# Attention on one core: two of ten probability chunks turned in 32x32 squares by VectorE and carried over DRAM, and the last query chunk weighed last

## The chip, the core and the metric

The kernel runs on one core of a Trainium2 chip. TensorE (PE in the profile; PEld is its weight load) multiplies into PSUM, VectorE (DVE) and ScalarE (ACT) read PSUM and SBUF, GpSimd (POOL) works on SBUF, and SyncE (SP) issues most of the transfers; the transfers run on 16 DMA engines. The metric is the device time of one execution in microseconds. The kernel before takes 2644.55 us, the median of three runs from 2643.07 to 2644.7.

## The reference

Everything is float32. A layer norm of x (4 batches of 512 tokens, 1024 wide) feeds an attention and a linear layer with routed low-rank additions; both are added to x. The attention has 32 query heads in 8 groups that share keys and values, head width 128, a causal mask, and a bias of minus slope times the root of the distance:

```python
xn = _layernorm(x)
qkv = xn @ w_qkv                      # q: 32 heads, k and v: 8 heads, 128 wide
scores = einsum('bqhgd,bkhd->bhgqk', q, k) * D ** -0.5
bias = -slopes * sqrt(max(rel, 0)), -inf where rel < 0      # rel = query - key
attn = softmax(scores + bias)
out = einsum('bhgqk,bkhd->bqhgd', attn, v).reshape(B, S, NH * D)
x = x + out @ w_o + (xn @ W.T + b + routed_low_rank(xn))
```

## The kernel before

There are three stages. *Projection* (`project`) makes q, k and v with two nested levels of a seven-product scheme for matrix multiplication and leaves them in DRAM. *Attention* (`attend`) works on them and writes its output, again as sums for such a scheme, to DRAM tensors `s`. *Finish* multiplies these by `w_o` and the linear layer's weights. The change is in attention.

Attention has 32 units (p, h, bi): two pairs of batches p, eight groups h, and within them the two batches bi of the pair. A unit has 4 heads and 512 tokens, cut into 4 chunks of 128. Query chunk i sees key chunks j = 0 to i, so a unit has ten (i, j) chunks. For each query chunk there are these steps:

- `scores(u, i)`: for each of the 4 heads, one product of queries by keys into one of three PSUM banks (L1014 on PE, (i+1)*128 columns); VectorE adds the bias, scales and finds the row's minimum (L1019); ScalarE takes exp and the row sum (L1023); VectorE inverts the sums (`tot`, L1026); GpSimd multiplies the rows `p3` to `p0` by them (L1028).
- `transpose_probs(u, i)`: each chunk (i, j) takes four 128x128 transposes on PE into one PSUM bank (L1039, `ptr`) and an eviction to a tile `pt`, by VectorE for even j (L1042) and by ScalarE for odd j (L1044).
- `weigh(u, i)`: PE multiplies the i+1 chunks by the values, 512 columns each (L1052), and ScalarE copies the result into `o` (L1053).
- `values(u)`: four transposes of the values (L1003).

One loop of the program handles a unit u and interleaves it with the scores of the next unit. Its order on PE is written out by hand: scores of the next unit for i=3, transposes of u for i=3; the same for i=2, then the next unit's values; scores i=1, weigh(u,3), transposes i=1; scores i=0, weigh(u,2), transposes i=0; weigh(u,1), weigh(u,0). The last unit has no next one; there a few products of the finish stage (`begin`) are put between.

When a pair of units (bi=0 and bi=1) is done, its outputs are summed for the finish stage: `outer_sums` makes three tiles `os` and one in place of `o`, four sums of 128x1024 on POOL (L130 and L133), done in the bi=0 loop of the next h. `middle_sums` then makes sums `ot` of them: of the `o` of bi=1 on POOL, in the same bi=0 loop, for the tensors (7, 4); of `os` on VectorE, for (5, 6, 3); of the `o` of bi=0 on VectorE, for (1, 2). Each set goes to DRAM by SP (L1105, L1106, L1116, L1118, L1119). For the last h but one `outer_steps` makes the `os` sums on VectorE.

`load` brings keys, queries and values (k, q, vT; L973 to L975) two units ahead. The orders of SP, VectorE, ScalarE and POOL in this stage are not written by hand: they come from the scheduler that builds the program and are fixed in it, an instruction after another for each engine. The tiles `p3` and so on exist twice, `pt` ten times, `o` four times, `os` once.

`homes[0]` is a pool of tiles of the finish stage, laid out already during attention; its tile `s1` (128 x 5 x 256) is used by operand sums of the finish stage.

Of the kernel before, what the change touches and what calls it, by code (L numbers as in the profile page):

```python
# [12 lines left out]
F32 = mybir.dt.float32  # L13
# [8 lines left out]
P = 128  # L22
NH, NKV, D = 32, 8, 128
G = NH // NKV
# [41 lines left out]
def kernel(  # L66
# [13 lines left out]
    nc = tc.nc  # L80
    B, S, H = x.shape
# [5 lines left out]
    HS = S // 2  # L87
    SCALE = D ** -0.5
    KB = 5
# [12 lines left out]
    dram = ctx.enter_context(tc.tile_pool(name="scratch", bufs=1, space=bass.MemoryType.DRAM))  # L102
# [837 lines left out]
            assert not (soon or later or weights or quiet or any(apart))  # L940


    def attend(front, begin):


        early = pool("bq", side="right")
        with ExitStack() as stack:
            sb, sq = None, early.__enter__()
            units = [(p, h, bi) for p in range(NP) for h in range(NKV) for bi in range(2)]
            sizes = {"dist": (S,), "q": (G, S), "k": (S,), "vT": (S,), "bias": (G, S)}  # L950
            counts = {"q": 2, "k": 2, "vT": 2, "v": 2, "pt": 10, "o": 4, "ot": 2}
            for i in (3, 2, 1, 0):
                sizes[f"p{i}"] = (G, (i + 1) * P)
                counts[f"p{i}"] = 2
            sizes.update(v=(NT, D), pt=(S,), os=(3, 2, S), o=(G, S), ot=(9, HS))
            queries = ("dist", "q", "k", "vT", "bias")

            def buf(tag, name):
                where = sq if tag in queries else sb
                return where.tile([P, *sizes[tag]], F32, tag=tag, name=name, bufs=counts.get(tag, 1))  # L960

            Q, K, VT, V, PR, O, bias = {}, {}, {}, {}, {}, {}, {}

            def label(u):
                return "_".join(str(k) for k in u)

            def load(u, queue=nc.sync):
# [19 lines left out]
                out=dist, in_=dist, compare_op=ALU.is_ge, fill=FAR,  # L987
# [10 lines left out]
            def values(u):  # L998
                n = label(u)
                V[u] = buf("v", f"v_{n}")  # L1000
                tr = bank("tr", f"v_{n}")
                for t in range(NT):
                    nc.tensor.transpose(tr[:, ts(t, P)], VT[u][:, ts(t, P)], ident)  # L1003
                nc.scalar.copy(V[u], tr.rearrange("p (t d) -> p t d", d=D))

            def scores(u, i):
                p, h, bi = u
                n = (i + 1) * P
                m = f"{label(u)}_{i}"
                tot = sb.tile([P, G], F32, tag=f"tot{i}", name=f"tot_{m}", bufs=2)  # L1010
                pr = PR[u, i] = buf(f"p{i}", f"p_{m}")
                for g in range(G):
                    sc = bank("sc", f"{m}_{g}")
                    nc.tensor.matmul(  # L1014
                        sc[:, :n], Q[u][:, g, ts(i, P)], K[u][:, :n], start=True, stop=True
                    )

                    low = sb.tile([P, 1], F32, tag=f"low{g}", name=f"low_{m}_{g}", bufs=2)
                    nc.vector.tensor_tensor_reduce(  # L1019
                        pr[:, g], sc[:, :n], bias[p, h][:, g, S - n :], -SCALE, BIG,  # L1020
                        ALU.add, ALU.min, low,
                    )
                    nc.scalar.activation(  # L1023
                        pr[:, g], pr[:, g], AF.Exp, bias=low, scale=-1.0, accum_out=tot[:, g : g + 1]
                    )
                nc.vector.reciprocal(tot, tot)  # L1026
                for g in range(G):
                    nc.gpsimd.tensor_scalar(  # L1028
                        pr[:, g], pr[:, g], tot[:, g : g + 1], 1.0, ALU.mult, ALU.mult
                    )  # L1030

            PT, OS = {}, {}

            def transpose_probs(u, i):
                for j in range(i + 1):
                    m = f"{label(u)}_{i}_{j}"
                    tr = bank("tr", m)
                    for g in range(G):
                        nc.tensor.transpose(tr[:, ts(g, P)], PR[u, i][:, g, ts(j, P)], ident)  # L1039
                    pt = buf("pt", f"pt_{m}")  # L1040
                    if j % 2 == 0:
                        nc.vector.tensor_copy(pt, tr)  # L1042
                    else:
                        nc.scalar.copy(pt, tr)  # L1044
                    PT[i, j] = pt

            def weigh(u, i):
                if u not in O:
                    O[u] = buf("o", f"o_{label(u)}")
                po = bank("o", f"{label(u)}_{i}")  # L1050
                for j in range(i + 1):
                    nc.tensor.matmul(po, V[u][:, j, :], PT[i, j], start=(j == 0), stop=(j == i))  # L1052
                nc.scalar.copy(O[u][:, :, ts(i, P)], po.rearrange("p (g k) -> p g k", k=P))  # L1053
# [87 lines left out]

            for tag in "ot os o p3 p2 p1 p0 v pt".split():
                buf(tag, f"lay_{tag}")
            for i in (3, 2, 1, 0):
                scores(units[0], i)
                if i == 3:
                    values(units[0])
            for n, u in enumerate(units):
                p, h, bi = u
                nxt = units[n + 1] if n + 1 < len(units) else None  # L1150
                after = units[n + 2] if n + 2 < len(units) else None
                if after:
                    load(after)
                if n == len(units) - 6:
                    front[0]()
                if not nxt:
                    early.__exit__(None, None, None)
                    front[1](O[p, h, 0])
                    fill = begin()
                if bi == 1:  # L1160
                    beside.append(middle_sums(p, h, (1, 2), "o", O[p, h, 0], True))
                for i in (3, 2, 1, 0):
                    if nxt:
                        scores(nxt, i)
                    if i > 1:
                        aside(outer, 1)
                    aside(below, 2)
                    if i < 2 or not nxt and i < 3 or n == close - 2 and i == 2:
                        aside(beside, 2)
                    if i < 2:  # L1170
                        weigh(u, i + 2)
                        if i == 0 and not nxt:
                            outer_sums(p, h, slice(HS, S))
                        next(fill, None)
                    transpose_probs(u, i)
                    next(fill, None)
                    if i == 2 and nxt:
                        values(nxt)
                    if i == 3:
                        aside(outer, 1)  # L1180
                    if not nxt:
                        if i == 3:
                            aside(beside, 2)
                        if i == 2:
                            while beside:
                                aside(beside, 1)
                        if i < 2:
                            front[3 - i]()
                if after and after[2] == 0:
                    distances(after)  # L1190
                aside(beside, 2)
                weigh(u, 1)
                next(fill, None)
                weigh(u, 0)
                if n == close:

                    while beside:
                        aside(beside, 1)
                for _ in fill:
                    pass  # L1200
                if bi == 1:
                    if n + 1 == close:
                        o = O[p, h, 1]
                        outer.append(outer_steps(p, h))
                        aside(outer, 1)
                        t = OS[p, h]
                    else:
                        o, t = outer_sums(p, h, slice(0, HS if (p, h) == last else S))
                        beside.append(pause(3))
                        for k in range(2):  # L1210
                            O.pop((p, h, k))
                        OS.pop((p, h))
                    below.append(middle_sums(p, h, (7, 4), "o", o, False))
                    beside.append(middle_sums(p, h, (5, 6, 3), "os", t, False))
# [427 lines left out]
    homes, begun = [], {}  # L1642
# [36 lines left out]
    with tc.manual_schedule(engines={PE, SP}):  # L1679
        attention = attend(  # L1680
            (
                lambda: bring(0, "w", *QUARTERS[:3]), second_home,
                lambda: (ops[1].weights(1), ops[1].weights(2)), lambda: ops[1].tokens(1),
            ),
            begin,
        )
        project(lambda: next(attention))
    with tc.manual_schedule(engines={PE}):
# [42 lines left out]
```

## Time and profile before

| | us |
|---|---|
| median of three runs | 2644.55 |
| the profiled execution | 2642.97 |
| its span, first to last instruction | 2641.2 |
| granted TensorE clock | 0.999 |

| stretch (us) | length | PE busy | DVE busy | ACT busy | POOL busy | DMA share | GB/s |
|---|---|---|---|---|---|---|---|
| 200 to 600 (projection) | 400 | 391.4 | 294.5 | 52.4 | 328.1 | 0.83 | 279 |
| 600 to 1080 (projection) | 480 | 475.7 | 334.5 | 34.1 | 411.5 | 0.72 | 246 |
| 1200 to 1400 (attention) | 200 | 198.6 | 136.0 | 135.7 | 149.8 | 0.67 | 218 |
| 1800 to 2641 (end of attention, finish) | 841 | 827.9 | 534.7 | 46.1 | 533.1 | 0.80 | 290 |

An engine's busy time is the time in which it had an instruction under way. The DMA share is the mean busy share of the 16 DMA engines. In timelines and groups, `po<-pt,v` reads "tile po written from tiles pt and v", x8 is eight instructions, and SPq stands for SP's queue, which issues transfers. A transfer's landing is the time from its issue until its data are there.

### The profile page before, as it was taken

How to read it: one execution, taken by the hardware profiler on the slowest of the kernel's cores; microseconds unless marked ns; L12 is line 12 of the kernel's file. 1: busy time of each engine (PE TensorE's matmuls, PEld its weight loads, DVE VectorE, ACT ScalarE, POOL GpSimd, SP SyncE). 2: the span in 40 equal slices, each digit the busy share in tenths (PEclk: the TensorE clock that was granted, in tenths of full speed). 3: DMA queues.
4: the chain of work that ended last, by engine and by line, in shares of the span. 5: the costliest groups of instructions: out<-in, count | busy, mean ns of one | idle time of the engine just before them, and what ended most of it. 6: DMA issues, size and time to landing. Idle time of an engine off the chain costs nothing.

```text
span 2641.2 us, 35979 instructions
## 1 busy us (share of the span) xinstructions
PE 2592.3 (98%) x11872; PEld 2069.8 (78%) x11872; DVE 1799.8 (68%) x3654; ACT 651.7 (25%) x1730; POOL 1924.0 (73%) x1976
## 2 busy tenths in 40 slices
PE   7999999999999999999999999999999999999999
PEld 6888888888888888856666665656788888888887
DVE  7776867867676677656666666676766666656574
ACT  3111111100000000366766766665000000000000
POOL 3687888877898988666877777684765566755593
PEclk9999999999999999999999999999999999999999
DMA  4479897869876776436566666757987878878884
GB/s 148 135 268 309 305 316 258 275 200 330 275 261 216 240 255 207 144 105 223 189 222 215 209 223 195 233 208 240 369 276 285 310 294 318 296 275 310 308 329 164
DMA packets 386570, 656.19 MB, mean 248 GB/s; under 512 B 22441, under 2 KB 291113, under 8 KB 376274
## 3 DMA queue, kind: packets, MB, share of 16 engines
q1 hardware_dynamic: 314322, 566.47, 61.8%
q10 hardware_dynamic: 70752, 82.85, 9.7%
q0 software_dynamic: 1312, 4.59, 0.5%
q8 instruction: 95, 1.56, 0.2%
q14 instruction: 89, 0.73, 0.1%
HBM read 392.72 MB, written 261.10 MB: 248 GB/s over the span
## 4 chain that ended last, share of the span: by engine, by line
PE 67%; POOL 3%; DVE 3%; DMA 2%; issue 1%; SPq 0%; ACT 0%; POOLq 0%; DVEq 0%; ACTq 0%
PE pc L1310 16%; PE psc L1014 9%; PE po L1052 9%; PE pd L1310 8%; PE pc_q L553 6%; PE pa L1310 4%; PE pc_kv L553 3%; PE ptr L1039 3%; PE pd_q L553 3%; PE pd_kv L553 2%; PE pa_q L553 1%; DVE p L1019 1%; DVE pt L1042 1%; PE pa_kv L553 1%; DMA s<-os 1%
## 5 line engine op out<-in xcount | busy, mean ns | idle before, releaser
L1028 POOL TENSOR_SCALAR p<-p,tot 128x256 f32<-128x256 f32 (+3 forms) x512 | 320.5, 648 | 136.8 <-DVE tot L1026 87.3
L1014 PE MATMUL psc<-k,q 128*128 128x512 f32 (+3 forms) x1024 | 306.2, 437 | 3.4 <-DVE low L1019 2.1
L1019 DVE CUSTOM_DVE_ANT_0 p<-psc,bias 128x256 f32<-128x256 f32 (+3 forms) x512 | 244.6, 490 | 93.6 <-PE psc L1014 71.2
L1023 ACT ACTIVATE p<-p,low 128x256 f32<-128x256 f32 (+3 forms) x512 | 283.8, 555 | 74.6 <-DVE low L1019 61.3
L1052 PE MATMUL po<-pt,v 128*128 128x512 f32 x640 | 290.9, 593 | 0.5 <-DVE pt L1042 0.5
L133 POOL TENSOR_TENSOR t<-w 128x640 f32<-128x640 f32 x95 | 186.3, 1961 | 135.6 <-DMA w<-m 58.9
L1014 PEld LDWEIGHTS psc<-k,q 128*128 128x128 f32 x1024 | 172.6, 190 | 102.7 <-issue 54.3
L133 POOL TENSOR_TENSOR t<-w,t 128x640 f32<-128x640 f32 x95 | 197.3, 2077 | 34.2 <-PE pc L1310 30.5
L1039 PEld LDWEIGHTS ptr<-ident,p 128*128 128x128 f32 x1280 | 147.3, 141 | 71.4 <-issue 40.1
L1052 PEld LDWEIGHTS po<-pt,v 128*128 128x128 f32 x640 | 116.6, 190 | 109.6 <-issue 99.6
L133 POOL TENSOR_TENSOR wr<-wr 128x256 f32<-128x256 f32 x220 | 173.1, 789 | 33.2 <-DMA wr<-in_w_o_dram 10.3
L1042 DVE COPY pt<-ptr 128x512 f32<-128x512 f32 x192 | 130.0, 683 | 75.8 <-PE ptr L1039 73.8
L1039 PE MATMUL ptr<-ident,p 128*128 128x128 f32 x1280 | 167.6, 274 | 4.3 <-DVE pt L1042 2.9
L553 PE MATMUL pc_q<-xi,ti_q 128*128 128x256 f32 x640 | 165.7, 381 | 2.9 <-DVE q L130 1.8
L168 ACT COPY m<-pc 128x256 f32<-128x256 f32 x30 | 11.2, 373 | 562.7 <-PE pc L1310 488.7
L133 DVE TENSOR_TENSOR wr<-wr 128x256 f32<-128x256 f32 x220 | 141.8, 645 | 7.6 <-DMA wr<-in_w_o_dram 4.0
L133 POOL TENSOR_TENSOR ti_q<-w_q 128x256 f32<-128x256 f32 x128 | 106.1, 829 | 56.0 <-PE pc_kv L553 32.9
L553 PEld LDWEIGHTS pc_q<-xi,ti_q 128*128 128x128 f32 x640 | 119.6, 190 | 24.5 <-issue 7.8
L553 PE MATMUL pd_q<-xi,ti_q 128*128 128x256 f32 x448 | 116.0, 381 | 5.6 <-POOL ti_q L133 5.6
L1310 PE MATMUL pc<-sa,w 128*128 128x256 f32 x480 | 113.8, 385 | 4.5 <-DMA sa<-s 4.5
L168 ACT COPY q<-pc_q 128x256 f32<-128x256 f32 x64 | 23.8, 372 | 357.1 <-PE pc_q L553 309.1
L1310 PE MATMUL pd<-s,w 128*128 128x256 f32 x480 | 111.5, 379 | 0.4 <-DVE s L133 0.4
(343 smaller groups left out, 6003.5 us busy)
## 6 DMA issues: line engine op xcount, KB each, us to landing
sa<-s SPq DMA_DIRECT2D x98, 640.0 KB, 8.1
s<-ot SPq DMA_DIRECT2D x107, 384.0 KB, 4.8
m<-wr SPq DMA_DIRECT2D x70, 512.0 KB, 4.7
w<-m SPq DMA_DIRECT2D x28, 1280.0 KB, 7.2
w_q<-in_w_qkv_dram SPq DMA_DIRECT2D x16, 2048.0 KB, 12.2
q<-q SPq DMA_DIRECT2D x32, 1024.0 KB, 7.2
s<-os SPq DMA_DIRECT2D x45, 512.0 KB, 4.8
t<-wr SPq DMA_DIRECT2D x40, 512.0 KB, 4.2
```

The source lines that it names most:

```text
L133: return eng.tensor_tensor(dst, u, v, ALU.subtract)
L168: nc.scalar.copy(dst, src)
L553: nc.tensor.matmul(dst, ops_w[m][:, c, :], XI[i][m][:, c, :], start=start and c == 0, stop=c == 1, skip_group_check=True,)
L1014: nc.tensor.matmul(sc[:, :n], Q[u][:, g, ts(i, P)], K[u][:, :n], start=True, stop=True)
L1019: nc.vector.tensor_tensor_reduce(pr[:, g], sc[:, :n], bias[p, h][:, g, S - n :], -SCALE, BIG, ALU.add, ALU.min, low,)
L1023: nc.scalar.activation(pr[:, g], pr[:, g], AF.Exp, bias=low, scale=-1.0, accum_out=tot[:, g : g + 1])
L1028: nc.gpsimd.tensor_scalar(pr[:, g], pr[:, g], tot[:, g : g + 1], 1.0, ALU.mult, ALU.mult)
L1039: nc.tensor.transpose(tr[:, ts(g, P)], PR[u, i][:, g, ts(j, P)], ident)
L1042: nc.vector.tensor_copy(pt, tr)
L1052: nc.tensor.matmul(po, V[u][:, j, :], PT[i, j], start=(j == 0), stop=(j == i))
L1310: nc.tensor.matmul(bk, w[:, k], x[:, k], start=start and k == 0, stop=stop and k == KB - 1, skip_group_check=True,)
```

## The change

In query chunk 3 the key chunks j = 0 and j = 2 are no longer transposed by PE. Instead, for the next unit:

- `turn_apart` has VectorE transpose the two chunks in squares of 32x32, within each group of 32 partitions, into a tile `px` (it lies in `homes[0]`'s `s1`); one SP transfer stores it in a DRAM tensor `turned_d`, 512 KB.
- `place_apart`, in the unit's own loop, has SP load the squares back in four transfers of 128 KB, each to 32 partitions, so that they lie in a tile `pd` (one buffer) as the transposed chunks; the 32 columns of a square are in a row, those of a head in four such rows.
- `weigh(u, 3)` takes these two chunks from `pd` and the others from `pt`. It moves from its place after the scores i=1 to the place after the transposes i=0; weigh(u,2) and weigh(u,1) move up one place. In the last unit it stays where it was.
- `pt` has eight buffers in place of ten.

The product, exp and sums are unchanged. Line numbers of the changed kernel differ: L1047 is the block transpose, L1051 the store, L1059 the loads, L1025 the reduction that was L1019, L1076 the eviction that was L1042, L1156 and L1157 the stores that were L1118 and L1119.

```diff
-            counts = {"q": 2, "k": 2, "vT": 2, "v": 2, "pt": 10, "o": 4, "ot": 2}
+            counts = {"q": 2, "k": 2, "vT": 2, "v": 2, "pt": 8, "o": 4, "ot": 2}
...
+            apart = ((0, 2),)
+            NA, SQ = sum(map(len, apart)), 32
+            NS = P // SQ
+            turned_d = dram.tile([2, P, NS, NA, G * SQ], F32, tag="turned_d", name="turned_d")
+            sizes["pd"] = (NS, NA, G, SQ)
...
+            def turn_apart(u, k):
+                px = homes[0].tile([P, KB, HS], F32, tag="s1", name=f"px_{label(u)}_{k}")
+                px = px.rearrange("p k c -> p (k c)")[:, : 2 * S].rearrange(
+                    "p (b n g i) -> p b n g i", n=2, g=G, i=SQ
+                )
+                for n, j in enumerate(apart[k]):
+                    nc.vector.transpose(
+                        out=px[:, :, n],
+                        in_=PR[u, 3][:, :, ts(j, P)].rearrange("p g (b c) -> p b g c", c=SQ),
+                    )
+                nc.sync.dma_start(
+                    out=turned_d[u[2]][:, :, ds(2 * k, 2)], in_=px.rearrange("p b n g i -> p b n (g i)")
+                )
+
+            def place_apart(u):
+                pd = buf("pd", f"pd_{label(u)}")
+                for b in range(NS):
+                    nc.sync.dma_start(
+                        out=pd[ds(b * SQ, SQ)].rearrange("c a n g i -> c a (n g i)"),
+                        in_=turned_d[u[2]][:, b].rearrange("(a c) n x -> c a (n x)", c=SQ),
+                    )
+                for n, j in enumerate(j for js in apart for j in js):
+                    placed[u, j] = pd[:, :, n].rearrange("p a g i -> p g a i")
...
             def transpose_probs(u, i):
                 for j in range(i + 1):
+                    if any(j in js for js in apart) and i == 3:
+                        continue
...
             def weigh(u, i):
+                if i == 3:
+                    for js in apart:
+                        for j in js:
+                            PT[i, j] = placed.pop((u, j))
...
+            for k in range(len(apart)):
+                turn_apart(units[0], k)
...
                     if i < 2:
-                        weigh(u, i + 2)
+                        weigh(u, i + 1 if nxt else i + 2)
...
                     transpose_probs(u, i)
+                    if i == (2 if nxt else 3):
+                        place_apart(u)
+                    if nxt and i < len(apart):
+                        turn_apart(nxt, len(apart) - 1 - i)
...
-                weigh(u, 1)
+                weigh(u, 3 if nxt else 1)
                 next(fill, None)
                 weigh(u, 0)
```

More of the change, by code (lines that the diff above doesn't have):

```diff
@@ L940, in project, with attend @@
             assert not (soon or later or weights or quiet or any(apart))
-    def attend(front, begin):
+    def attend(front, begin, homes):
         early = pool("bq", side="right")
@@ L1030, in scores @@
                     )
-            PT, OS = {}, {}
+            PT, OS, placed = {}, {}, {}
+            def turn_apart(u, k):
[20 more added lines that the diff above has]
+                    placed[u, j] = pd[:, :, n].rearrange("p a g i -> p g a i")
             def transpose_probs(u, i):
                 for j in range(i + 1):
+                    if any(j in js for js in apart) and i == 3:
+                        continue
                     m = f"{label(u)}_{i}_{j}"
@@ L1143, in attend @@
                 buf(tag, f"lay_{tag}")
+            buf("pd", "lay_pd")
             for i in (3, 2, 1, 0):
@@ L1684 @@
             ),
-            begin,
+            begin, homes,
         )
```

## The prediction

> **What bounds the kernel now.** I read the engine shares first, then busy time by stage, then one pair of units engine by engine. The busy line, and from the view by stages a stretch of attention (columns: stretch, length, busy time and instructions of PE, PEld, DVE, ACT and POOL, clock, DMA share, GB/s):
>
> ```profile
> PE 2592.3 (98%) x11872; PEld 2069.8 (78%) x11872; DVE 1799.8 (68%) x3654; ACT 651.7 (25%) x1730; POOL 1924.0 (73%) x1976
> 1400.00:1600.00 200.00, 198.27 (x831) 120.40 (x830) 132.93 (x398) 136.02 (x376) 154.58 (x181) 1.00 0.63 202
> ```
>
> TensorE sets the pace of attention too: 198.3 of 200 us at full clock. POOL, with 155 us, comes next. Now TensorE through one whole loop, that of a unit with bi=0 (timeline: start, length, instructions):
>
> ```profile
> 1390.78 3.60 PE L1014 MATMUL psc<-k,q 128*128 128x512 f32 x8
> 1394.22 2.21 PE L1039 MATMUL ptr<-ident,p 128*128 128x128 f32 x16
> ...
> 1402.52 3.60 PE L1052 MATMUL po<-pt,v 128*128 128x512 f32 x8
> 1405.96 1.04 PE L1039 MATMUL ptr<-ident,p 128*128 128x128 f32 x8
> ...
> 1408.04 2.74 PE L1052 MATMUL po<-pt,v 128*128 128x512 f32 x6
> 1410.62 0.60 PE L1039 MATMUL ptr<-ident,p 128*128 128x128 f32 x4
> 1411.06 2.74 PE L1052 MATMUL po<-pt,v 128*128 128x512 f32 x6
> 1413.63 3.60 PE L1014 MATMUL psc<-k,q 128*128 128x512 f32 x8
> ```
>
> The loop lasts 22.85 us. I count times from its first score matmul (+0 = 1390.78). Consecutive starts give 0.86 us for a 512-wide product and 0.43 us for a chunk's four transposes (1410.62 to 1411.06). The same stretch on POOL, then on SP:
>
> ```profile
> 1391.88 2.37 POOL L130 TENSOR_TENSOR os<-o 128x1024 f32<-128x1024 f32 x1 [2.68 <-DMA s<-os]
> ...
> 1399.09 2.37 POOL L133 TENSOR_TENSOR os<-o,os 128x1024 f32<-128x1024 f32 x1
> 1401.45 2.69 POOL L1028 TENSOR_SCALAR p<-p,tot 128x512 f32<-128x512 f32 x4
> ...
> 1410.16 1.28 POOL L133 TENSOR_TENSOR o<-o 128x512 f32<-128x512 f32 x1
> ```
>
> ```profile
> 1400.96 0.32 SPq L975 DMA_DIRECT2D vT<-v  x1
> 1411.46 0.37 SPq L1118 DMA_DIRECT2D s<-o  x1
> 1411.88 0.50 SPq L1119 DMA_DIRECT2D s<-ot  x1
> 1412.44 1.01 SPq L1118 DMA_DIRECT2D s<-o  x1
> 1413.49 1.13 SPq L1119 DMA_DIRECT2D s<-ot  x1
> 1414.72 1.31 SPq L973 DMA_DIRECT2D k<-k  x1
> ```
>
> In bi=0 loops POOL has four sums of the pair before (os), the normalisation of p3 and four sums of ot in one chain, from +1.1 to +20.7. SP stands for it: between vT and L1118 it issues nothing. From the waits of the DMA queue (total, times, longest) and the DMA issues (median us to landing):
>
> ```profile
> SPq L1118 <- POOL o L133: 143.0, 13, 19.5
> k<-k SPq DMA_DIRECT2D x26, 256.0 KB, 4.4
> ```
>
> Today nothing behind that wait is urgent: k and q are for a unit two loops on.
>
> **The change, part by part.** *Removed:* per unit eight PE transposes (two chunks of 0.43 us) and two DVE evictions L1042 (0.68 us each). If PE is the only limit, 32 x 0.87 = 27.7 us are gained. *Moved:* weigh(u,2) and weigh(u,1) one place forward, weigh(u,3) to the end. The same ten products run, so this alone costs nothing on PE.
>
> *Added on DVE:* two block transposes of 128x512 per unit. The trace has none. The nearest rows are the 128x512 eviction (0.68) and the 128x512 sum from SBUF (0.71, L130/L133); I take 0.69, with 0.29 (a 128x128 L1019) and 1.29 (a 128x768 sum) as ends. The amount replaces the two evictions; the place is what costs. In the changed order of DVE the first transpose stands between the two copies pt of T(2) (transposes of query chunk 2) and waits for POOL's p3 of the next unit. Behind it in DVE's order stand the copy pt_2_2, which weigh(u,2) needs, and the L1025 reductions that empty the three score banks.
>
> In bi=0 loops p3 is ready at 1404.14 = +13.4. So: transpose to +14.1, copy +15.0, first reduction +15.5, the fourth 256-wide score +16.0. The weighing starts there, where it starts at +11.7 now: 4.3 us late. The following DVE work (second transpose, two ot sums of 1.29 and 1.12, copy of pt_1_0) ends at +20.7, weigh(u,1) starts at +21.2 against +17.3 for its place now: 4.0 us late. In bi=1 loops POOL has no sums. There p3 takes 2.7 us after its reciprocal (about +5.9), so +8.8; the same steps bring the weighing to +11.4 against 11.8 now, and the later ones gain up to 0.9. I take a gain of 0.6 in each of 15 such loops, of the 0.87 that PE saves: -9 us. With 1.29 for the transpose that gain is gone.
>
> *Added on SP:* per unit one store of 512 KB (L1051) and four loads of 128 KB (L1059). Order decides here. The changed SP order, around a bi=0 unit:
>
> ```
> 660 L979 DMACopy k_4_0_13248<-k_4_122 128x512
> 661 L980 DMACopy q_4_0_13249<-q_4_100 128x2048
> 662 L1059 DMACopy pd_3_0_13352<-turned_d 32x4x256 x3
> 663 L1156 DMACopy s_149<-o_2_1_13159 128x4x256
> 664 L1157 DMACopy s_149<-ot_2_7_13281 128x3x256
> 665 L1156 DMACopy s_150<-o_2_1_13159 128x4x256
> 666 L1157 DMACopy s_150<-ot_2_7_13281 128x3x256
> 667 L1059 DMACopy pd_3_0_13352<-turned_d 32x4x256
> 668 L1051 DMACopy turned_d<-px_3_1_0_13449 128x1024
> ```
>
> Three of four pieces of pd go out, then come the four stores that wait for POOL's ot chain (L1118/L1119 before), then the fourth piece. weigh(u,3) needs all four. So the fourth is issued where k is issued today: 1414.72 = +23.9, after +20.7 for POOL and the four issues. A piece of 128 KB is not in the trace; the rows are vT with 256 KB in a quiet queue (2.5 at least), k behind these very stores (4.4), q with 1 MB (7.2). I take k: landed at +28.3. PE would reach weigh(u,3) at +21.2 + 1.7 + 0.4 = +23.4, so it stands 4.9 us more. Then five products (4.3): the next loop starts at +32.6 instead of +22.85, **+9.8 us**. POOL's chain starts anew each pair, on stores and the pair's last o, so this comes back every time. In bi=1 loops no such stores stand ahead; pd's four loads go out when the late weigh(u,3) ends and land some 6 us into the loop, ten before use. Behind the fourth piece stand px of the next unit and k, q, vT: each is needed at +8 of the next loop or later, and I cost that at nothing.
>
> Loops: the split order stands in 12 bi=0 units (p=0, h=2 to 7; p=1, h=0 to 4 and 6): 12 x 9.8 = 117.6. At p=1, h=5 all four pieces stand behind the stores, three more issues of about 1.2: 13.3. At p=0, h=1 they stand ahead; only DVE's wait counts: 4.0. The first bi=0 loop has no sums: -1; the last has p3 at +10.7 (timeline: 4.56 from 1808.88, loop at 1802.76): +1. The last unit's loads stand behind six os stores and the sa and w loads, which now end issue at 1843.5, while its weighing starts at 1831.86. With one store more (about 1) and a landing of 4.4 that is 17 us late; ends are 0, if those loads move forward, and 25.
>
> Sum: 117.6 + 13.3 + 4.0 - 1 + 1 + 17 - 9 = +143. The profiled execution took 2642.97 us (span 2641.2, 1.8 around it), 1.6 below the median of the runs; so **2786 us**.
>
> *DMA traffic:* 1 MB per 22 us, 46 GB/s on 202 at a share of 0.63, gives about 0.77: not full, but landings grow, which the upper end takes in.
>
> *The turned operand:* weigh(u,3) now reads pd in runs of 32 elements. No row shows a product with such runs; every moving operand here has 128 or more in a row. Ends: nothing, or twice the time of two products, 1.7 us in each of 32 units, 55 us. The products' time is the same per column for 256 and 512 (0.43 and 0.86), which says nothing against runs; I take nothing.
>
> [...] The trace has 0.43 us for a chunk's four transposes on PE, beside an eviction. [...]
> k lands after 4.4 us here. [...]
>
> **Rivals.**
> *Faster.* The fourth piece lands in time and p3 is ready by +8.8 in every loop: PE's saving stands, 2643 - 27 = 2616. This needs POOL's chain done by about +9 instead of +20.7, less than half its 19.5 us of work; only a POOL that does the sums later could, and its changed order is the old one. 5%.
> *Only DVE's wait.* The loads are not late, or SP issues sooner: 14 x 4.0 - 9 = +47, 2690. For it: the wait on p3 alone is certain by the order. Against: the fourth piece stands behind the stores in 12 units. 10%.
> *Strided reads double.* The forecast plus 55: 2841. 12%.
> *Slow landings.* Pieces land after 7.2 like q: 13 x 2.8 = 36 more, 2822. 15%.
>
> **How the numbers follow.** Forecast 56%, the rivals as given, 2% for no change at all or worse than all of these. The range reaches from landings of 2.5 us and no lateness at the end (2786 - 25 - 17, and some 6 for a bi=1 gain of 1.0) to strided reads: 2738 to 2845. It leaves out the first two rivals, 15%, and tails. What a measurement can tell from no change is 0.2%, 5.3 us: faster 5%, within 1%, slower 94%.
>
> **What would show it.** Right: bi=0 loops of about 32 us and bi=1 of 22; the first product of weigh(u,3) waiting on the pd load for some 5 us, DVE standing 4 us before the transpose for POOL's p3, SP still waiting for POOL at L1156. Wrong: equal loops below 22 us; products from pd longer than 0.86 us; pd landing before the four stores.

## The result and the profile after

| | before | after |
|---|---|---|
| median of the runs, us | 2643.81 (2640.22 to 2644.7, 4 runs) | 2845.1 (2840.98 to 2850.92, 4 runs) |
| ratio, with its 95% interval | | 1.0766 (1.0744 to 1.0788) |
| profiled execution, us | 2642.97 | 2840.98 |
| span, us | 2641.2 | 2839.2 |
| granted TensorE clock | 0.999 | 0.966 |

The changed kernel is 7.7% slower: 198 us in the profiled executions, where the forecast said 143. The median lies 0.1 us above the upper end of the range.

First the busy line of the page and the same stretch of attention as before the change (columns: stretch, length, busy time and instructions of PE, PEld, DVE, ACT and POOL, clock, DMA share, GB/s):

```profile
PE 2625.0 (92%) x11616; PEld 2067.4 (73%) x11616; DVE 1778.1 (63%) x3654; ACT 643.4 (23%) x1730; POOL 1928.0 (68%) x1976
1400.00:1600.00 200.00, 160.72 (x571) 91.66 (x572) 98.15 (x302) 100.20 (x283) 117.58 (x136) 0.88 0.60 197
```

Nothing is full any more: in 200 us TensorE is busy for 160.7, and every other engine for less than before. So the loss is waiting. One thing is odd: TensorE executes 256 instructions fewer in the whole run, worth 27.7 us, and is busy for 32.7 us *more*. Some 60 us of its work got slower, and the clock of 0.88 says why.

Now TensorE through the second half of one bi=0 loop, which starts at 1212.35 (timeline: start, length, instructions; in brackets the idle time before and what ended it):

```profile
1227.82 1.22 PE L1020 MATMUL psc<-k,q 128*128 128x256 f32 x2 [5.20 <-DVE low L1025]
1228.83 4.41 PE L1090 MATMUL po<-pt,v 128*128 128x512 f32 x6
...
1235.06 1.88 PE L1090 MATMUL po<-pt,v 128*128 128x512 f32 x4
1236.78 0.60 PE L1073 MATMUL ptr<-ident,p 128*128 128x128 f32 x4
1242.68 2.05 PE L1090 MATMUL po<-pd,v 128*128 128x512 f32 x2 [5.31 <-DMA pd<-turned_d]
1244.52 1.68 PE L1090 MATMUL po<-pt,v 128*128 128x512 f32 x2
1246.04 1.02 PE L1090 MATMUL po<-pd,v 128*128 128x512 f32 x2
...
1248.61 3.60 PE L1020 MATMUL psc<-k,q 128*128 128x512 f32 x8
```

Two idle times of 5.2 and 5.3 us, one for VectorE, one for the load of pd, as forecast. The loop lasts 36.26 us (22.85 before). But behind each idle time the products are slow: weigh(u,2) takes 4.41 us for its six instructions, which took 2.74 before, and the first two products of weigh(u,3) stand 1.84 and 1.52 us apart instead of 0.86.

What held them, on VectorE, POOL and SP:

```profile
1226.07 0.71 DVE L1047 STREAM_TRANSPOSE px<-p 128x512 f32<-128x512 f32 x1 [5.46 <-POOL p L1034]
...
1230.06 1.04 DVE L130 TENSOR_TENSOR ot<-os 128x768 f32<-128x768 f32 x1
1231.14 1.22 DVE L133 TENSOR_TENSOR ot<-ot,os 128x768 f32<-128x768 f32 x1
```

```profile
1213.80 2.37 POOL L130 TENSOR_TENSOR os<-o 128x1024 f32<-128x1024 f32 x1 [3.00 <-DMA s<-os]
...
1223.36 2.69 POOL L1034 TENSOR_SCALAR p<-p,tot 128x512 f32<-128x512 f32 x4
...
1228.59 2.96 POOL L1034 TENSOR_SCALAR p<-p,tot 128x384 f32<-128x384 f32 x4
1231.53 1.96 POOL L133 TENSOR_TENSOR ot<-o,ot 128x512 f32<-128x512 f32 x1
1233.44 1.27 POOL L133 TENSOR_TENSOR o<-o 128x512 f32<-128x512 f32 x1
```

```profile
1216.39 1.67 SPq L1059 DMA_DIRECT2D pd<-turned_d  x3
1234.74 0.38 SPq L1156 DMA_DIRECT2D s<-o  x1
...
1237.96 1.27 SPq L1059 DMA_DIRECT2D pd<-turned_d  x1
```

VectorE stands 5.46 us in front of the block transpose until POOL's p3 is done (1223.36 + 2.69). SP issues three pieces of pd, stands until POOL's chain ends at 1234.7, and issues the fourth behind the four stores; the first product from it starts 4.7 us after that issue.

And the clock, in the view by stages, of the two idle times and what follows each (the number ahead of the last two is the clock):

```profile
1222.62:1227.80 5.18, 0.00 (x1) 0.00 (x0) 1.73 (x6) 0.00 (x0) 5.10 (x7) 0.76 0.14 27
1227.80:1232.50 4.70, 4.68 (x7) 2.38 (x8) 3.93 (x10) 2.19 (x8) 4.70 (x6) 0.53 0.00 0
...
1237.30:1242.60 5.30, 0.08 (x1) 0.00 (x0) 0.69 (x1) 1.83 (x4) 0.91 (x3) 0.98 1.03 342
1242.60:1246.00 3.40, 3.32 (x4) 1.51 (x5) 0.00 (x0) 0.00 (x0) 0.00 (x0) 0.52 0.98 267
```

Behind the two idle times the clock is granted at about half, 0.53 over 4.70 us and 0.52 over 3.40 us; in the stretches after that (1232.50 to 1237.30 and 1246.00 to 1248.60) it is at 1.00. The forecast had no such term.

The loops tell the rest. Loops with bi=1 take 22.14 us (22.84 before). The one bi=0 loop with POOL's sums whose four loads stand ahead of the stores takes 28.67; the thirteen in which loads stand behind them take 34.8 to 40.6, 36.62 in the mean. The last unit waits once, for its pd:

```profile
2029.98 2.05 PE L1090 MATMUL po<-pd,v 128*128 128x512 f32 x2 [22.24 <-DMA pd<-turned_d]
```

### The profile page after: what moved, and what is told of

Read it like the earlier page. It is cut to its first block, busy times and chain, and to the rows that moved or that the text cites. A ratio compares the mean times of both kernels' runs of the same rounds, so it can differ in the third digit from the quotient of the medians.

```text
span 2839.2 us, 35643 instructions
## 1 busy us (share of the span) xinstructions
PE 2625.0 (92%) x11616; PEld 2067.4 (73%) x11616; DVE 1778.1 (63%) x3654; ACT 643.4 (23%) x1730; POOL 1928.0 (68%) x1976
## 3 DMA queue, kind: packets, MB, share of 16 engines
q8 instruction: 93, 1.52, 0.2%
## 4 chain that ended last, share of the span: by engine, by line
PE 56%; POOL 8%; DMA 5%; DVE 4%; issue 4%; SPq 2%; ACT 1%; DVEq 0%; POOLq 0%; ACTq 0%
PE pc L1355 14%; PE po L1090 9%; PE pd L1355 7%; PE pc_q L553 5%; PE psc L1020 5%; PE pa L1355 4%; POOL p L1034 3%; PE pc_kv L553 3%; DMA pd<-turned_d 3%; PE pd_q L553 3%; PE pd_kv L553 2%; PE ptr L1073 2%; PE pa_q L553 1%; ACT p L1029 1%; DMA q<-q 1%
## 5 line engine op out<-in xcount | busy, mean ns | idle before, releaser
L1025 DVE CUSTOM_DVE_ANT_0 p<-psc,bias 128x256 f32<-128x256 f32 (+3 forms) x512 | 240.9, 489 | 260.7 <-PE psc L1020 246.7
L1020 PE MATMUL psc<-k,q 128*128 128x512 f32 (+3 forms) x1024 | 320.8, 448 | 83.7 <-DVE low L1025 82.0
L1090 PE MATMUL po<-pt,v 128*128 128x512 f32 x512 | 276.7, 668 | 0.0
L1090 PEld LDWEIGHTS po<-pt,v 128*128 128x128 f32 x512 | 110.6, 221 | 118.1 <-issue 99.9
L1090 PE MATMUL po<-pd,v 128*128 128x512 f32 x128 | 82.1, 729 | 89.7 <-DMA pd<-turned_d 45.5
L1073 PEld LDWEIGHTS ptr<-ident,p 128*128 128x128 f32 x1024 | 120.0, 141 | 60.6 <-issue 46.5
L1091 ACT COPY o<-po 128x512 f32<-128x512 f32 x128 | 74.9, 586 | 290.1 <-PE po L1090 289.4
L1073 PE MATMUL ptr<-ident,p 128*128 128x128 f32 x1024 | 132.9, 273 | 0.1
L1076 DVE COPY pt<-ptr 128x512 f32<-128x512 f32 x128 | 86.9, 679 | 62.0 <-PE ptr L1073 62.0
```

The lines of the kernel that those rows point to most:

```text
L1020: nc.tensor.matmul(sc[:, :n], Q[u][:, g, ts(i, P)], K[u][:, :n], start=True, stop=True)
L1025: nc.vector.tensor_tensor_reduce(pr[:, g], sc[:, :n], bias[p, h][:, g, S - n :], -SCALE, BIG, ALU.add, ALU.min, low,)
```

## The experiments

Each kernel ran on one chip beside the kernel before; every ratio is to it, with its 95% interval. Times are medians. The changed kernel's 2845.1 us is 202 above the 2642.88 that the kernel before took beside runs 1 to 4.

**1. The loads of pd ahead of the waiting stores.** `pin` keeps an instruction behind all that the program put on its engine earlier; with it SP issues all four loads before L1156 in every bi=0 loop.

```diff
-                    if i == (2 if nxt else 3):
+                    if i == 3:
                         place_apart(u)
...
-                    nc.sync.dma_start(out=pd...
+                    pin(nc.sync.dma_start(out=pd...
```

> Only the order on SP differs: the four loads of pd stand ahead of the stores that wait for POOL's ot chain, in every unit. My theory (two waits in turn, the SP wait the greater): the 13 loops of 36.6 us become like the one loop of the changed kernel whose loads stand ahead already (28.7 us), 13 x 7.9 = 103 us less: about 2742, within 2725 and 2765; TensorE still stands some 5 us before the weighing of query chunk 2, and no longer before the products from pd. Rival 1 (VectorE's wait for p3 is the cost and what follows it comes with it): no more than 1% below the changed kernel, 2815 to 2845. Rival 2 (the landings of pd are slow in themselves, by 6 us or more): the wait before pd stays, above 2800.

Measured: 2751.12 us, 1.0414 (1.0397 to 1.0432). TensorE in the same loop, then SP:

```profile
1228.04 1.22 PE L1020 MATMUL psc<-k,q 128*128 128x256 f32 x2 [5.17 <-DVE low L1025]
1229.05 4.38 PE L1090 MATMUL po<-pt,v 128*128 128x512 f32 x6
...
1237.40 1.02 PE L1090 MATMUL po<-pd,v 128*128 128x512 f32 x2
1238.26 1.02 PE L1090 MATMUL po<-pt,v 128*128 128x512 f32 x2
```

```profile
1216.65 2.33 SPq L1059 DMA_DIRECT2D pd<-turned_d  x4
1234.97 0.38 SPq L1156 DMA_DIRECT2D s<-o  x1
```

The time is within the range expected. The wait for pd is gone (there is no bracket at 1237.40; of the fourteen loops one still has such a wait, of 1.9 us), the loop takes 29.1 us, and 94 us of the 202 went with nothing but the place of the loads on a queue. The wait for VectorE stays, and so do 21.3 us in the last unit. The products from pd follow at 0.86 us here: the reads in runs of 32 cost nothing, and those at 1.84 in the changed kernel were the clock (0.52).

**2. The block transposes at the end of the loop.** The two `nc.vector.transpose` are pinned; they come behind the last copy pt instead of between the copies of T(2). Nothing else was edited, but the scheduler now also puts three of four loads of pd behind the stores, not one.

> Only the order on VectorE differs: the two block transposes stand at the end of the loop, behind the last copy pt, so nothing of TensorE's work waits behind them. My theory: the weighing of query chunk 2 starts at +11.7 again, but the fourth load of pd still stands behind the stores, issued at some +23.5 and landed at +28, so TensorE only waits longer there, some 9 us; a split loop is +28 + 1.7 + 4.3 = 34 us instead of 36.6, 13 x 2.6 = 34 less and 6 for the one loop without the split: about 2805, within 2785 and 2825. Rival (VectorE's wait is the cost): 14 loops x 5.8 = 81 us less, 2764 or below.

Measured: 2845.31 us, 1.0769 (1.0753 to 1.0785), the same as the changed kernel; neither number was met. SP and TensorE in a loop that starts at 1265.88:

```profile
1286.40 0.37 SPq L1156 DMA_DIRECT2D s<-o  x1
...
1289.61 3.03 SPq L1059 DMA_DIRECT2D pd<-turned_d  x3
```

```profile
1295.47 2.04 PE L1090 MATMUL po<-pd,v 128*128 128x512 f32 x2 [12.19 <-DMA pd<-turned_d]
```

No wait for VectorE is left, weighing starts on time, and TensorE then stands 12 to 20 us for pd, where it stood 4 to 8. The end of a loop is set by POOL's chain, the stores and the loads behind them, whatever TensorE has done by then. The expectation named that longer wait and undersized it: it missed the two further loads of about 1 us each, and took 4.3 us for the five products behind the wait, which take 6.8 from 1295.47 to 1302.24, behind 12.19 us of idle time. The rival, that VectorE's wait is the cost, asked for 81 us less and is out: even with the two later loads and the slower products added back, an estimate of 2 and 1 us in each of 13 loops from the rows above, it comes to some 40. What its removal is worth with exactly one load behind the stores, no run shows; with all loads ahead of them it is 73 us (run 3 against run 1).

**3. Both.**

> Both orders changed: the loads of pd ahead of the waiting stores and the block transposes at the end of the loop. My theory (the two waits are all of the loss, the turning and its traffic cost nothing by themselves): all loops near 22.1 us, 32 x 0.7 = 22 less than before, and some 20 us more for the last unit, whose loads still stand behind others: 2625 to 2660, by the working 2642. Rival (what is added costs by itself: reads of pd in runs of 32, traffic at a share of 0.77, VectorE's added work): well above, 2690 or more, with loops of 24 us also where no wait is left.

Measured: 2677.7 us, 1.0135 (1.012 to 1.015): 167 of the 202 us are gone, so the two waits hold most of the loss between them, though the runs that took out one of them gave back 94 and nothing. The time lies between the two expected ranges, 2625 to 2660 and 2690 or more. Loops without a wait take 21.54 to 21.61 us, 1.3 less than before the change; 0.87 had been forecast for them. The other 35 us stand in the waits of TensorE (total, times, longest) and in SP's queue:

```profile
PE po L1090 <- DMA pd<-turned_d: 61.7, 12, 25.6
```

```profile
1225.50 0.38 SPq L1156 DMA_DIRECT2D s<-o  x1
...
1228.77 1.23 SPq L1051 DMA_DIRECT2D turned_d<-px  x1
...
1234.17 2.27 SPq L1059 DMA_DIRECT2D pd<-turned_d  x4
```

25.6 us is the last unit. The other 36.1 fall on eleven loops. Nine of them wait for 1 to 2.7 us: now the *store* of px stands behind the four stores that wait for POOL, and the next unit's loads can't start before it has landed (5.4 us from 1228.77 to 1234.17). Two late ones wait 10.5 and 8.0 us; there five loads of the finish stage, or six stores of the os sums, stand ahead of pd's loads on SP. 31 loops x 1.3 = 40 gained, 61.7 waited, the remaining 13 of the 35 are, by estimate, mostly slower products behind the waits (up to 2.05 us for two instructions, 1.02 otherwise): five of these eleven loops are 2.0 to 2.7 us longer than the wait and a quiet loop make together. The rival, that the added work costs by itself, is out for the loops without a wait.

**4. No idle time ahead of weigh(u,3).** The test of the clock: work is added.

```diff
+                if nxt and bi == 0 and n > 2:
+                    spare = bank("tr", f"spare_{label(u)}")
+                    for g in range(36):
+                        nc.tensor.transpose(spare[:, ts(g % G, P)], PR[u, 0][:, g % G, :P], ident)
                 weigh(u, 3 if nxt else 1)
```

> Work is added: in the bi=0 loops 36 spare transposes of 0.11 us on TensorE, some 3.9 us, in the idle time ahead of weigh(u,3), into a bank that nobody reads. Theory (after an idle time of some 5 us the clock is granted at about half for 3.4 to 4.7 us, and the first products after it lose 1.7 us; without the idle time they don't): 13 x 1.7 = 22 us less than the changed kernel, about 2823, the clock in the products from pd 1.00 instead of 0.52. Rival 1 (the first products are slow because of pd, its reads or its neighbours on the DMA engines): the products from pd stay at 2.05 us for two, time 2845 or more. Rival 2 (added work on TensorE only adds): 2845 + up to 13 x 3.9 = 2895.

Measured: 2821.73 us, 1.0678 (1.0662 to 1.0694), 23.4 us *below* the changed kernel with 504 transposes more. One loop on TensorE, and its clock while weigh(u,3) runs:

```profile
1241.94 4.09 PE L1240 MATMUL ptr_spare<-ident,p 128*128 128x128 f32 x36
1247.30 1.10 PE L1090 MATMUL po<-pd,v 128*128 128x512 f32 x2 [1.26 <-DMA pd<-turned_d]
1248.24 1.02 PE L1090 MATMUL po<-pt,v 128*128 128x512 f32 x2
```

```profile
1247.30:1251.67 4.37, 4.37 (x10) 1.98 (x11) 0.00 (x0) 0.58 (x1) 0.00 (x0) 1.00 0.88 300
```

Still the load comes last, but the products behind it run at a clock of 1.00 and stand 0.94 and 0.86 apart. In the profiled executions the thirteen loops that had waited for pd take 35.1 us in the mean, where they took 36.6: 1.5 us each came back. In the changed kernel the clock is 0.53 over 4.70 us behind an idle time of 5.20 us, and 0.52 over 3.40 us behind one of 5.31. In run 3 slow products, 1.38 to 2.05 us for two instructions where 1.02 to 1.10 is usual, also follow waits of 2.31, 2.46 and 2.65 us (last section); what the clock was there is not shown.

**5. The order of weighing alone.** In the kernel before, weigh(u,3) goes to the end and the others one place forward; all chunks are turned by TensorE.

> The kernel before with one part of the change alone: weigh(u,3) last and the two others one place forward; all ten chunks are turned by TensorE and pt keeps its ten buffers. Theory (the order alone costs nothing and gains nothing; the 1.3 us by which the loops without waits are shorter than before come from the eight transposes, 0.87, and from the wait for a bank between the sixteen of query chunk 3, 0.43): 2643, within 5 us. Rival (the order gives the 0.43 by itself): 31 x 0.43 = 13 less, about 2630.

Measured: 2645.07 us, 1.0005 (0.9995 to 1.0014). The order costs and gains nothing. So nearly all of the 1.3 us of a quiet loop come from the transposes. The sixteen of query chunk 3 that start at 1394.22 in the kernel before took 2.05 us, until its next score product; the eight left take 0.87 in run 3, 1.18 us less. The first line is of the kernel before, the others of run 3:

```profile
1396.27 2.75 PE L1014 MATMUL psc<-k,q 128*128 128x384 f32 x8
1183.44 1.04 PE L1073 MATMUL ptr<-ident,p 128*128 128x128 f32 x8
1184.31 2.75 PE L1020 MATMUL psc<-k,q 128*128 128x384 f32 x8
```

**6 to 8. The store, then the loads too, on ScalarE's queue.** Run 6 is run 3 with `nc.scalar.dma_start` for the store of px, pinned. Run 7 also leaves the last unit's ten chunks to TensorE. Run 8 is run 7 with the loads of pd on ScalarE, issued behind the copies of query chunk 2.

> As the kernel with both orders changed, and the store of px is issued by ScalarE behind the block transposes at the end of the loop, so it no longer stands on SP behind the stores that wait for POOL. Theory: the 2 to 3 us that eleven loops still wait for pd are the late store's; they go, with the slow products after them: 2677.7 - 36 - some 8 = about 2634, within 2625 and 2645; the last unit still waits some 25 us. Rival (pd's loads land late by the added traffic, whoever issues the store): 2670 to 2680.

> As the run with the store on ScalarE, and the last unit's ten chunks are all turned by TensorE, as before the change, since nothing covers the way of its chunks over memory. Theory: the last unit's wait of some 25 us goes and 1.3 comes back: 2634 - 24 = about 2610, within 2600 and 2622, 1.2% faster than the kernel before. Rival (that wait is covered elsewhere, the finish stage starts no earlier): about 2634.

> As the run before it (last unit turned by TensorE, block transposes at the end of the loop, store on ScalarE), and the four loads of pd are issued by ScalarE too, behind the copies of query chunk 2, some 10 us ahead of their use; SP issues what it issued before the change. Theory (the loops wait for pd only because its loads share SP with transfers that wait for others): the 38 us of waits go and some 6 us of slow products, 2662 - 44 = about 2618, faster than the kernel before by 1%. Rival (the shorter loops meet POOL's chain: its first sum waits for the stores of os, and a pair of units can't go below what POOL and these stores take, some 45 us as before): 2640 to 2662, with the waits in other places.

Measured: 2686.48 us (1.0165, 1.0151 to 1.0179), 2662.39 (1.0071, 1.0058 to 1.0083) and 2704.37 (1.0223, 1.0209 to 1.0238). The last unit's 24 us came back as expected (run 7 against run 6); none of the three met its range. In run 6 TensorE still waits 60.2 us for pd in 14 places, now and then for VectorE's reductions too (14.5 us), and POOL's first sum of os starts later and later in its loop (1.6, 4.2 and 5.5 us after the start in three bi=0 loops in a row), having waited for the stores of os. The trace shows where the lateness comes back: in the bi=1 loops with a wait of 1 to 2.7 us, SP's four stores behind POOL's chain go out 3.6 to 6.0 us after the start of the loop, where they went out after 2.1 to 2.9 in run 3; k, q and vT follow, and the four loads start after 10.0 to 12.5 us, hardly before the 10.9 to 12.8 of run 3. What the store on ScalarE saved, the later chain took. In run 8 the wait stands elsewhere, as the waits of TensorE and ScalarE's queue show:

```profile
PE po L1090 <- ACT pt L1078: 58.1, 13, 7.7
```

```profile
1391.73 4.70 ACTq L1059 DMA_DIRECT2D pd<-turned_d  x4
```

In 14 of the 31 loops ScalarE takes more than 4 us to get four loads out, at most 7.7, and 1.8 to 3.6 in the others; its copies pt stand behind them: the wait has moved from SP's queue to ScalarE's. The four issues themselves take 1.5 of the 4.7 us shown; the other 3.1 lie between the first and the second load, and 3.3 more passed idle ahead of the first. What held ScalarE there no run shows.

**9 and 10. Only where no store has to pass the wait.** Run 9 is run 3 with only the bi=0 units turned by VectorE: those are turned and stored in a bi=1 loop, where SP has no store waiting for POOL's ot chain, and loaded ahead of the stores in their own. Run 10 leaves out one more unit; this is its edit against run 3:

```diff
+            turned = lambda u: u[2] == 0 and u != units[-6]
...
-                    if i == 3:
+                    if i == 3 and turned(u):
                         place_apart(u)
-                    if nxt and i < len(apart):
+                    if nxt and turned(nxt) and i < len(apart):
                         turn_apart(nxt, len(apart) - 1 - i)
```

> As the kernel with both orders changed, but only the 16 units with bi=0 have two chunks turned by VectorE; those with bi=1 are as before the change, weighing order included. A bi=0 unit's squares are turned and stored in a bi=1 loop, where POOL has no sums, and loaded ahead of the stores that wait; none has to be stored behind that wait, and the last unit (bi=1) waits for none. Theory: no wait for pd is left and each bi=0 loop is 1.3 us shorter: 2643 - 16 x 1.3 = about 2622, within 2612 and 2632, 0.8% faster than the kernel before. Rival (a pair of units can't be shorter than POOL's sums and the stores of os allow, some 45.7 us as before): 2643, within 5.

> As the run before it, with the unit (1, 5, 0) left to TensorE too: its loop is the only one that still waited for pd (6.8 us, and some 2 us of slow products), since two large loads of the finish stage go out ahead of its own. Theory: 9 less, 2635 - 9 = about 2626, within 2620 and 2632. Rival (a later stage gives it back): 2635, within 3.

Measured: 2635.29 us (0.9965, 0.9952 to 0.9979) and 2629.28 us (**0.9944, 0.9931 to 0.9958**). Run 9 lies between its two expected ranges, 2612 to 2632 and 2638 to 2648; run 10 is within its own and beats both kernels, by 0.6% against the kernel before. Its loops, one turned and one not, alternate on TensorE:

```profile
1649.52 3.60 PE L1020 MATMUL psc<-k,q 128*128 128x512 f32 x8
...
1671.06 3.60 PE L1020 MATMUL psc<-k,q 128*128 128x512 f32 x8
...
1693.88 3.60 PE L1020 MATMUL psc<-k,q 128*128 128x512 f32 x8
```

21.54 us and 22.82: the whole 1.3 per turned unit. 15 x 1.3 = 19.5 were to be had, 14.6 came; short waits of 1 to 2 us for VectorE late in the stage, as at 1735.86 (2.16 us), are part of the rest. Run 9's own 6.8 us of waiting in the loop of (1, 5, 0) went as expected.

## Why the prediction was right and wrong

The mechanism was the forecast one, and each wait stood where it was put. Where the steps of one split loop ended, from the loop's start, in us:

| step | forecast | loop at 1212.35 |
|---|---|---|
| POOL's p3 ready, first block transpose | +13.4 | +13.7 |
| weigh(u,2) starts | +16.0 | +16.5 |
| weigh(u,1) starts | +21.2 | +22.7 |
| POOL's chain done | +20.7 | +22.4 |
| fourth piece of pd issued | +23.9 | +25.6 |
| its data there, first product from pd | +28.3 | +30.3 |
| next loop | +32.6 | +36.3 |

*The first step that failed* is "Then five products (4.3): the next loop starts at +32.6". The row of 0.86 us a product is from a TensorE that was busy for 198.3 of 200 us, at a clock of 1.00; the prediction put 5 us of idle time ahead of it and kept the row's duration. Behind the wait the five take 5.9 us in this loop (the clock is 0.52 over the first 3.40) and 6.3 in the mean of the twelve split loops. Run 4 shows the clock as cause: with most of the idle time filled they take 4.4 us at a clock of 1.00 in the loop shown, and 1.5 us a loop came back. The same happens at weigh(u,2) (4.41 us, not 2.74), but in split loops TensorE then waits for pd anyway; it counts only in the loop at p=0, h=1 (28.67, forecast 26.85).

*The second* is a size: "after +20.7 for POOL". The chain ends 1.7 later in this loop and 1.5 in the mean of the twelve. Here it starts 0.35 later, and p3 with it; and its last p2 and ot sum take 2.96 and 1.96 us instead of 2.27 and 1.28, in this loop beside VectorE's 128x768 sums at 1230.06 and 1231.14. In run 2, in the loop where those sums come after POOL's two (1285.15 against 1281.65 to 1285.15), the two take the old durations (the first two rows):

```profile
1281.65 2.26 POOL L1034 TENSOR_SCALAR p<-p,tot 128x384 f32<-128x384 f32 x4
1283.88 1.27 POOL L133 TENSOR_TENSOR ot<-o,ot 128x512 f32<-128x512 f32 x1
1285.12 1.26 POOL L133 TENSOR_TENSOR o<-o 128x512 f32<-128x512 f32 x1
1285.15 2.04 DVE L130 TENSOR_TENSOR ot<-os 128x768 f32<-128x768 f32 x1
```

The last two rows run side by side, and here it is VectorE's sum that takes longer, 2.04 us where it took 1.04 in the changed kernel. In both loops one of the two sums that ran side by side was the longer; that the overlap is the cause was not shown, as no run moved the sums alone.

*The landing* taken from k, 4.4, was near: 4.7 from the issue of the fourth piece to its product in this loop, 3.7 in the median of all pieces. "Slow landings" is out.

The sum, with what was measured: twelve split loops +13.4 each, 160.6 (forecast 9.8, 117.6); p=1, h=5 +17.8 (13.3); p=0, h=1 +5.8 (4.0); the first and the last bi=0 loop -0.7 and +3.0 (-1, +1); the last unit +23.2, of which 22.2 is the wait (17); fifteen bi=1 loops -0.7 each, -10.9 (-9); the rest of the run -0.8. Together 198. So 43 of the 55 us that were missing are the twelve loops, 3.6 us each: in their mean 2.0 in the products behind the wait, 1.5 in POOL's chain, the rest in issue and landing. The last unit, put at 17, adds 6.

*The rivals.* "Strided reads double" ended at 2841, close to the measured time, and is wrong: where TensorE had not waited, the products from pd stand 0.86 us from the next (run 1, from 1237.40). "Only DVE's wait", 2690, is what run 1 makes true, and it took 2751: the wait costs 6.7 us a loop in the mean of the fourteen, not 4.0, 1.6 of it slower products in the loop shown (weigh(u,2) takes 4.38 us, not 2.74), and the last unit's 21 us weren't in that sum. "Faster" asked for a POOL chain done by about +9; that was never needed, as it is enough that nothing urgent stands behind it. With the split removed and the transposes late, the gain a loop is 1.3 us, more than the 0.87 taken.

*The turning and moving* cost nothing by themselves in the loops of runs 3 and 10 that don't wait (21.54 to 21.61 us in run 3, 21.54 in the loop shown of run 10, where 22.85 stood before the change); the price is where the transfers stand in the queues.

## What to carry to other kernels

Before a step goes from an engine to a transfer, go through the queue that will issue it and ask of each instruction ahead of it what it waits for: here four stores that nobody needed soon held up a load, and moving the loads ahead of them gave back 7 us in each of thirteen loops. When two waits stand in one loop, don't price them one by one; the run that removed one gave 94 us, the run that removed the other, in which two more loads came late, nothing, and both together 167. And price the work behind a new wait of TensorE at the clock measured behind such a wait (here 0.53 and 0.52 behind 5.20 and 5.31 us), not by rows from where it was busy (1.00).

## What the runs showed of the hardware

In the changed kernel TensorE's clock was 0.53 for 4.70 us behind an idle time of 5.20 us, and 0.52 for 3.40 us behind one of 5.31. In run 4, with 36 spare transposes (4.09 us) in the idle time ahead of weigh(u,3), it was 1.00 over the 4.37 us behind them in the loop shown, and the time was 2821.73 us instead of 2845.1. Slow products also stood behind a shorter idle time, in these rows of run 3 from the second product on:

```profile
1425.42 1.10 PE L1090 MATMUL po<-pd,v 128*128 128x512 f32 x2 [2.65 <-DMA pd<-turned_d]
1426.36 1.82 PE L1090 MATMUL po<-pt,v 128*128 128x512 f32 x2
1427.97 1.91 PE L1090 MATMUL po<-pd,v 128*128 128x512 f32 x2
```

After 2.65 us of idle time the two instructions of the first product take 1.10 us, and those of the next two, from 0.94 us later, 1.82 and 1.91. Behind another wait, of 2.31 us, in that run the first product took 2.05 us; behind one of 2.46 the first two took 1.38 and 1.92, behind one of 2.44 they took 1.10 and 1.02: no fixed limit can be read from these.

A block transpose of 128x512 float32 in squares of 32x32 took VectorE 0.71 us in the changed kernel (median of 64), about as long as a copy of that size (0.69). A product from pd, whose moving operand is in runs of 32 elements, and the one from pt behind it took 1.02 us each in run 1, 0.86 from one start to the next.
